# A recurrent layer with a gate: products of h added in PSUM onto x Wx and onto each other, a plain first step, and the gate's two layers moved

## The chip, the cores and the metric

The kernel runs on one core of a Trainium2 chip. The metric is the device time of one execution in microseconds (us). Before the change it is 3159.95 us, the median of three runs (3158.42 to 3160.47). The engines are named as in the profile: PE (TensorE), DVE (VectorE), ACT (ScalarE), POOL (GpSimd) and SP (SyncE, which here only issues DMAs).

## The reference

Layer 0 is a recurrence over 256 steps for 64 rows of width 1024, layer 1 a gate computed from the condition vector alone. All of it is float32.

```python
xW = jnp.einsum('ntd,dh->nth', x, Wx) + b          # x: (64, 256, 1024)
next_h = jnp.tanh(prev_h @ Wh + xw)                # 256 steps, h0 = cond
x = x + h_t
h = jax.nn.silu(cond @ W1.T + b1)
gate = jax.nn.sigmoid(h @ W2.T + b2)[:, None, :]
# v: a Haar transform over time, all coefficients times the gate, and its inverse
x = x + (v + a)
```

The transform is linear and its coefficients are all scaled by the same gate, so layer 1 is x times (2 + gate). The kernel calls that `factor`.

## The kernel before

Constants: S = 2 steps make a pair, NP = 128 pairs, T = 256 steps; P = 128, R = 32, Q = 4, B = 8, KB = 4, G = 2, W = 512, E = 128, D = 1024.

**x Wx.** For each pair of steps, `XWork` splits x into a high part x0, a rest x1 and a mixed part x2 (DVE lines 112, 244 and 246, ACT cast at line 252). PE multiplies them with three parts of Wx, 48 matmuls of 128 x 512 per pair (line 228). `first()` does the 16 "mixed" ones and 8 of "main", `second()` the other 24. ACT and POOL then take the mixed sums (lines 260 and 261, `+ b_row`), DVE adds the main sums (line 295), the pair goes to DRAM (`sum_d`, line 299) and comes back rearranged as xW of two steps (line 305, eight DMAs, four for each step), all issued by SP.

**h Wh.** Each step is a Strassen product in blocks of halves: seven products of 16 matmuls each (`strassen_product`, line 172; each float32 matmul stands as two records in the profile). The four column groups of the array work side by side on 32 columns of weights each. The weight sides are made once by `strassen_weight` (lines 159 to 162), the sides of h in every step by `strassen_sides` (lines 185 to 188). `h_product` runs products 1, 7, 5, 6, then 4, 3, 2. In PSUM, parts 7, 5, 4, 3 and 2 share the bank `three`, while m1 and m6 have their own. ACT copies m1 and the parts 5 and 7 out (lines 202 and 204), POOL makes four additions with xW (lines 208, 209, 210 and 213), DVE two more (lines 212 and 214), and line 218 adds `three` to y. Tanh is on ACT (line 392), the transposition of h on DVE (line 394).

**The loop.** For even steps PE gets, after the step's products, `second()` of the next pair; for odd steps `first()` of the pair after that. So between the last product of a step and the first of the next, PE has 24 matmuls of x Wx. Then POOL adds h to x (line 409).

**The gate.** In steps 0 to 7, `gate_product` adds one of eight blocks of the first layer (a load of a W1 slab and 8 matmuls of 256 columns, 16 records in the profile), in steps 8 to 15 the second layer. `gate_hidden` follows step 7 and `gate_factor` step 15. The biases b1 and b2 are loaded by ACT into the buffer of h0 (tag h0T), which has one copy.

**The output.** Until `factor` exists the first eight pairs are stored in DRAM (`kept`). Later pairs are scaled by POOL (line 379) and stored to yT. In pairs 9 to 16 the kept slabs are loaded, scaled on POOL and stored, one per pair.

**Preparation.** Ahead of the loop, x0 to x2 and the slabs of Wx and Wh are loaded by SP. Each Wx slab is split by DVE, ACT and, for odd k, POOL (`split_weight`, lines 112 and 123 to 126). Six buffers of 512 KB (tag slab) hold x, raw Wx and the gate's weights in turn.

The program names engines and data; a planner of the framework puts the instructions of each engine in order by its own costs, starting from the written order, and adds all waits. In the quiet pairs PE keeps the written order. In the preparation it doesn't: products of step 0 stand between blocks of x Wx. Several DVE instructions of `XWork` stand among the sides of h.

## Time and profile before

| quantity | value |
|---|---|
| median of 3 runs | 3159.95 us |
| profiled execution, in all | 3156.64 us |
| its span | 3154.8 us |
| mean granted PE clock | 0.995 |
| busy PE / DVE / ACT / POOL | 3098.7 / 2070.4 / 632.5 / 1703.2 us |
| moved by DMA | 303.85 MB, mean 96 GB/s |

The profile is of one execution. A row of a timeline has the start in us, the length in us, engine, line, operation, output and inputs, shapes and count, and in brackets the engine's idle time before it with what ended it. The chain of waits goes back from the last instruction to what released each one, and lists the pieces in order of time. A window row gives the stretch, its length, then the busy us (and instructions) of PE, PEld, DVE, ACT and POOL, the granted clock, the DMA share and GB/s.

### The profile page before, as it was taken

The page shows a single profiled execution, that of the slowest core. Times are in us where ns is not written, and L with a number is a line of the kernel's source. Part 1 is how long each engine was busy: PE and PEld are TensorE (multiplying, and loading weights), DVE is VectorE, ACT ScalarE, POOL GpSimd, SP SyncE. Part 2 cuts the span into 40 slices and gives each one's busy share as a digit, 9 for nine tenths or more (in the row PEclk, how much of TensorE's full clock was granted, in tenths as well). Part 3 has the DMA queues.
Part 4 walks back from the last instruction along what each step waited for, and adds up shares of the span by engine and source line. Part 5 has one row for each costly group of instructions (what it writes and reads, how often), then busy time and mean ns, then how long its engine had stood idle before and what let it go on. Part 6 is the DMA issues. An engine that isn't in the chain of part 4 may idle for free.

```text
span 3154.8 us, 138243 instructions
## 1 busy us (share of the span) xinstructions
PE 3098.7 (98%) x63744; PEld 2699.4 (86%) x63744; DVE 2070.4 (66%) x2722; ACT 632.5 (20%) x1172; POOL 1703.2 (54%) x1808
## 2 busy tenths in 40 slices
PE   6999999999999999999999999999999999999998
PEld 4878788888888888888888888888888888888887
DVE  7556566666676666666666666666666766666665
ACT  3111112122122122112211211221221211212121
POOL 4335655555555555555555555555555555555554
PEclk8999999999999999999999999999999999999999
DMA  5334332222222222222222222222222222222221
GB/s 185 128 118 143 120 116 95 90 89 90 96 82 95 95 84 93 93 89 89 89 96 83 93 93 89 90 95 90 89 89 96 83 94 96 85 90 95 90 74 65
DMA packets 145763, 303.85 MB, mean 96 GB/s; under 512 B 23584, under 2 KB 89632, under 8 KB 145184
## 3 DMA queue, kind: packets, MB, share of 16 engines
q1 hardware_dynamic: 144128, 293.69, 27.6%
q8 instruction: 500, 8.19, 1.1%
q10 hardware_dynamic: 1056, 1.31, 0.1%
q14 instruction: 79, 0.65, 0.1%
HBM read 156.50 MB, written 138.41 MB: 93 GB/s over the span
## 4 chain that ended last, share of the span: by engine, by line
PE 91%; DMA 2%; DVE 2%; issue 1%; POOL 1%; ACT 0%; SPq 0%; POOLq 0%; DVEq 0%; ACTq 0%
PE three L172 34%; PE main L228 28%; PE mixed L228 15%; PE m L172 14%; DMA kept_x<-kept 1%; DMA yT<-x 1%; PE ps_g L340 0%; DVE s L185 0%; POOL kept_x L379 0%; DVE x L244 0%; POOL x L409 0%; POOL y L213 0%; DVE hT L394 0%; DMA b_n<-b 0%; DMA sum_d<-sum 0%
## 5 line engine op out<-in xcount | busy, mean ns | idle before, releaser
L228 PE MATMUL main<-wx,x 128*128 128x512 f32 x4096 | 996.7, 395 | 19.0 <-ACT wx L123 14.6
L228 PEld LDWEIGHTS main<-wx,x 128*128 128x128 f32 x4096 | 759.9, 188 | 204.2 <-issue 26.8
L409 POOL TENSOR_TENSOR x<-x,hT 128x512 f32<-128x512 f32 x256 | 462.3, 1806 | 864.8 <-DVE hT L394 853.6
L172 PE MATMUL three<-wh,s 128*32 128x128 f32 x16320 | 544.6, 273 | 8.1 <-DVE s L185 5.7
L228 PE MATMUL mixed<-wx,x 128*128 128x512 f32 x2048 | 506.4, 399 | 1.3 <-DVE wx L126 0.9
L172 PEld LDWEIGHTS three<-wh,s 128*32 128x32 f32 x16320 | 459.0, 110 | 11.9 <-issue 10.6
L228 PEld LDWEIGHTS mixed<-wx,x 128*128 128x128 f32 x2048 | 375.7, 188 | 102.2 <-issue 25.8
L212 DVE TENSOR_TENSOR u<-m,c 128x128 f32<-128x128 f32 x256 | 74.5, 291 | 439.1 <-PE m L172 433.5
L392 ACT ACTIVATE h<-h 128x512 f32<-128x512 f32 x256 | 161.9, 633 | 1000.0 <-DVE h L218 1000.0
L218 DVE TENSOR_TENSOR h<-three,y 128x384 f32<-128x384 f32 x256 | 142.7, 558 | 334.5 <-PE three L172 304.0
L261 POOL TENSOR_TENSOR sum<-sum,b_row 128x512 f32<-128x512 f32 x256 | 341.7, 1336 | 6.2 <-ACT sum L260 6.2
L379 POOL TENSOR_TENSOR x<-x,factor 128x512 f32<-128x512 f32 x240 | 329.8, 1374 | 9.5
L394 DVE STREAM_TRANSPOSE hT<-h 128x512 f32<-128x512 f32 x256 | 182.0, 711 | 177.5 <-ACT h L392 177.5
L209 POOL TENSOR_TENSOR y<-c 128x128 f32<-128x128 f32 x256 | 127.3, 497 | 310.2 <-ACT c L204 310.2
L172 PEld LDWEIGHTS m<-wh,hT 128*32 128x32 f32 x8160 | 210.2, 110 | 94.0 <-issue 87.5
L172 PE MATMUL m<-wh,hT 128*32 128x128 f32 x8160 | 276.9, 277 | 6.9 <-DVE hT L394 6.8
L246 DVE SCALAR_TENSOR_TENSOR x<-x,x_high 128x1024 fp32r<-128x1024 f32 x128 | 282.6, 2208 | 0.0
L172 PE MATMUL three<-wh,hT 128*32 128x128 f32 x8160 | 274.8, 273 | 1.0 <-issue 0.4
L172 PE MATMUL m<-t,s 128*32 128x128 f32 x8160 | 269.8, 273 | 5.2 <-DVE s L187 5.2
L172 PE MATMUL three<-t,hT 128*32 128x128 f32 x8160 | 270.9, 273 | 2.0 <-ACT c L204 1.6
L172 PE MATMUL three<-t,s 128*32 128x128 f32 x8160 | 269.9, 273 | 0.0
L214 DVE TENSOR_TENSOR h<-y,u 128x128 f32<-128x128 f32 x256 | 202.0, 789 | 88.5 <-POOL y L210 87.5
(63 smaller groups left out, 3190.3 us busy)
## 6 DMA issues: line engine op xcount, KB each, us to landing
x<-xT SPq DMA_DIRECT2D x128, 512.0 KB, 3.8
sum_d<-sum SPq DMA_DIRECT2D x128, 512.0 KB, 3.0
xw<-sum_d SPq DMA_DIRECT2D x1024, 64.0 KB, 2.0
yT<-x SPq DMA_DIRECT2D x120, 512.0 KB, 2.8
wx<-wx SPq DMA_DIRECT2D x8, 512.0 KB, 7.0
wh<-wh SPq DMA_DIRECT2D x8, 512.0 KB, 5.8
w<-w1T SPq DMA_DIRECT2D x8, 512.0 KB, 3.9
kept<-x SPq DMA_DIRECT2D x8, 512.0 KB, 2.6
```

Source lines behind the costliest of these rows:

```text
L172: nc.tensor.matmul(out=out[q * R : (q + 1) * R], lhsT=a[:, k * R : (k + 1) * R], rhs=wh_s[i][k][:, q], start=first and k == 0, stop=k == K ...
L209: nc.gpsimd.tensor_add(y22, c57[:, 0], c57[:, 1])
L212: nc.vector.tensor_add(u, m6, c1)
L214: nc.vector.tensor_add(pre[:, 3], y22, u)
L218: nc.vector.tensor_add(pre[:, :3].rearrange("p i e -> p (i e)"), three[:, : 3 * E], y[:].rearrange("p i e -> p (i e)"))
L228: nc.tensor.matmul(out=acc[h], lhsT=v[:, k * P : (k + 1) * P], rhs=wx_s[k][which][:, h * HALF : (h + 1) * HALF], start=start and k == 0, s ...
L246: nc.vector.scalar_tensor_tensor(out=self.x2, in0=self.x1[:].bitcast(F32), scalar=-UP, in1=self.high, op0=ALU.mult, op1=ALU.add)
L261: nc.gpsimd.tensor_add(s, s, b_row[:, h * HALF : (h + 1) * HALF])
L379: nc.gpsimd.tensor_mul(v, v, blocks(factor))
L392: nc.scalar.activation(h, h, AF.Tanh)
L394: nc.vector.transpose(hT, h)
L409: nc.gpsimd.tensor_add(x_step(t), x_step(t), blocks(hT))
```

## The change

- `h_product` gets a PSUM bank `acc` into which ACT has copied xW of the step (`put`). Products 2, 4 and 3 are added onto it. Product 6 is added onto product 1 in the bank `m16`, after ACT has copied product 1 out to y0; ACT then copies the sum to u. Products 5 and 7 stand side by side in the bank `m57`. DVE makes y1, y2 and y3 from them and u, and one addition over 512 columns makes h. The four POOL additions, the copies c1 and c57 and the DVE sum of 128 columns are gone. The order of products is 1, 2, 5, 6, 7, 4, 3.
- Step 0 has a plain product of h0 with the raw Wh (64 matmuls of 256 columns) instead of a Strassen one; the Strassen sides of Wh are made afterwards, all on DVE.
- In the preparation, each of eight rounds loads a slab of Wx and one of W1 (SP) and one of Wh (ACT), splits Wx (the subtraction always on DVE), and gives PE a block of x Wx and a block of the gate's first layer.
- The gate's second layer is in steps 0 to 7; b1 has its own buffer, b2 that of h0. Three pairs are kept instead of eight; each is loaded in a pair with i % 4 = 0 and scaled in the next.
- Pairs are scaled by step. The last two steps are added and scaled by DVE in halves, with two stores on two queues.

```diff
-    def split_weight(w: bass.AP) -> list:
-        out = []
-        for k in range(B):
...
-            three = [wpool.tile([P, D], F32R, tag=f"wx{i}", name=f"wx{i}_{k}") for i in range(3)]
-            nc.scalar.copy(three[0], w0)
-            (nc.gpsimd if k % 2 else nc.vector).tensor_sub(raw, raw, w0)
...
-            out.append(three)
-        return out
-    def load_bias(v: bass.AP, name: str):
-        t = const.tile([P, G, F], F32, tag="h0T", name=name)
+    def split_weight(raw, k: int) -> list:
...
+        nc.scalar.copy(three[0], w0)
+        nc.vector.tensor_sub(raw, raw, w0)
...
+        return three
+    def load_bias(v: bass.AP, pool, tag: str, name: str):
+        t = pool.tile([P, G, F], F32, tag=tag, bufs=1, name=name)
...
-    def strassen_weight(raw: dict) -> dict:
+    def strassen_weight(raw: list) -> dict:
...
-            nc.gpsimd.tensor_sub(t1, b12, b11)
-            nc.gpsimd.tensor_sub(b12, b22, b12)
+            nc.vector.tensor_sub(t1, b12, b11)
+            nc.vector.tensor_sub(b12, b22, b12)
             nc.vector.tensor_sub(t2, b22, t1)
             nc.vector.tensor_sub(t4, b21, t2)
...
-    def strassen_product(out, a, i: int, first: bool) -> None:
+    def strassen_product(out, a, i: int, first: bool = False) -> None:
...
+    def plain_product(ps, vT, w, k: int) -> None:
+        for g in range(G):
+            col = (g * B + k) * R
+            for q in range(Q):
+                nc.tensor.matmul(
+                    out=ps[q * R : (q + 1) * R, g * F : (g + 1) * F],
+                    lhsT=vT[:, col : col + R],
+                    rhs=w[:, q * F : (q + 1) * F],
+                    start=k == 0 and g == 0,
+                    stop=k == B - 1,
+                    skip_group_check=True,
+                    tile_position=(0, q * R),
+                )
...
-    def h_product(a: dict, xw, t: int):
-        three = bank("three", f"three{t}")
-        m1, m6 = (bank(f"m{i}", f"m{i}_{t}")[:, :E] for i in (1, 6))
-        part = [three[:, i * E : (i + 1) * E] for i in range(3)]
-        pre = work.tile([P, 4, E], F32, tag="h", bufs=1, name=f"h{t}")
-        strassen_product(m1, a[1], 1, True)
-        strassen_product(part[2], a[7], 7, True)
-        strassen_product(part[1], a[5], 5, False)
-        strassen_product(m6, a[6], 6, True)
-        c1 = sums.tile([P, E], F32, tag="c1", name=f"c1_{t}")
-        nc.scalar.copy(c1, m1)
-        c57 = sums.tile([P, 2, E], F32, tag="c57", name=f"c57_{t}")
-        nc.scalar.copy(c57[:].rearrange("p i e -> p (i e)"), three[:, E : 3 * E])
-        y = sums.tile([P, 3, E], F32, tag="y", name=f"y{t}")
-        y22 = sums.tile([P, E], F32, tag="y22", name=f"y22_{t}")
-        nc.gpsimd.tensor_add(y[:, 0], c1, xw[:, 0])
-        nc.gpsimd.tensor_add(y22, c57[:, 0], c57[:, 1])
-        nc.gpsimd.tensor_add(y22, y22, xw[:, 3])
+    def flat(v):
+        return v[:].rearrange("p i e -> p (i e)")
+    def put(xw, t: int):
+        acc = bank("acc", f"acc{t}")
+        nc.scalar.copy(acc, flat(xw))
+        return acc
+    def h_product(acc, a: dict, t: int):
+        m16, m57 = (bank(f"m{i}", f"m{i}_{t}") for i in (16, 57))
+        m16, m5, m7 = m16[:, :E], m57[:, :E], m57[:, E : 2 * E]
+        part = [acc[:, i * E : (i + 1) * E] for i in range(3)]
+        y = sums.tile([P, 4, E], F32, tag="y", bufs=1, name=f"y{t}")
         u = sums.tile([P, E], F32, tag="u", name=f"u{t}")
-        nc.vector.tensor_add(u, m6, c1)
-        nc.gpsimd.tensor_add(y[:, 1:3], xw[:, 1:3], u[:].unsqueeze(1).broadcast_to((P, 2, E)))
-        nc.vector.tensor_add(pre[:, 3], y22, u)
-        strassen_product(part[2], a[4], 4, False)
-        strassen_product(part[1], a[3], 3, False)
-        strassen_product(part[0], a[2], 2, False)
+        strassen_product(m16, a[1], 1, True)
+        nc.scalar.copy(y[:, 0], m16)
+        strassen_product(part[0], a[2], 2)
+        strassen_product(m5, a[5], 5, True)
+        strassen_product(m16, a[6], 6)
+        nc.scalar.copy(u, m16)
+        strassen_product(m7, a[7], 7)
         nc.vector.tensor_add(
-            pre[:, :3].rearrange("p i e -> p (i e)"), three[:, : 3 * E], y[:].rearrange("p i e -> p (i e)")
+            y[:, 1:3], m57[:, : 2 * E].rearrange("p (i e) -> p i e", i=2), u[:].unsqueeze(1).broadcast_to((P, 2, E))
         )
-        return pre[:].rearrange("p i e -> p (i e)")
+        nc.vector.tensor_add(y[:, 3], m7, y[:, 1])
+        strassen_product(part[2], a[4], 4)
+        strassen_product(part[1], a[3], 3)
+        h = work.tile([P, W], F32, tag="h", bufs=1, name=f"h{t}")
+        nc.vector.tensor_add(h, acc, flat(y))
+        return h
     def bank(tag: str, name: str):
         return one_pool.tile([P, HALF], F32, tag=tag, name=name)
...
+        def block(self, k: int) -> None:
+            for h in range(2):
+                x_matmul(self.main, self.x0, 0, h, k, start=True)
+            for h in range(2):
+                x_matmul(self.main, self.x1, 1, h, k, stop=True)
+            for h in range(2):
+                x_matmul(self.mixed, self.x2, 2, h, k, True, True)
         def first(self) -> None:
             self.begin()
...
     nc.scalar.dma_start(out=h0T, in_=condT)
     b_row = const.tile([P, D], F32, tag="b_row", name="b_row")
-    nc.scalar.dma_start(out=b_row, in_=b.broadcast_to((P, D)))
     load_x(0)
     now = XWork(0)
-    wx_s = split_weight(wx)
+    now.begin()
+    gate_ps = bank("gate", "gate_ps1")
+    wx_s, wh_raw = [], []
+    for k in range(B):
+        raw = slab(f"wx{k}")
+        nc.sync.dma_start(out=raw, in_=wx[k])
+        w1 = slab(f"w1_{k}")
+        nc.sync.dma_start(out=w1, in_=w1T[k])
+        wx_s.append(split_weight(raw, k))
+        now.block(k)
+        plain_product(gate_ps, h0T, w1, k)
+        wh_raw.append(wpool.tile([P, D], F32, tag="wh", name=f"wh_{k}"))
+        nc.scalar.dma_start(out=wh_raw[k], in_=wh[k])
+        if k == 0:
+            nc.scalar.dma_start(out=b_row, in_=b.broadcast_to((P, D)))
+    b1_n = load_bias(b1, sums, "y", "b1_n")
     load_x(1)
-    wh_raw = load_by_halves(wh)
     load_x(2)
-    now.by_blocks()
+    now.take_mixed()
     xw_next = now.finish()
-    now = XWork(1)
-    now.first()
-    wh_s = strassen_weight(wh_raw)
-    gate_ps = {}
...
+    def gate_hidden(z):
+        nc.vector.tensor_add(z, gate_ps, z)
...
-    early = 2 * B // S
-    kept = [dram.tile([P, D], F32, tag="kept", bufs=early, name=f"kept{i}") for i in range(early)]
-    hT = h0T
-    sides = strassen_sides(hT, -1)
-    factor = None
+    def of_step(x, s: int):
+        return x[:].rearrange("p (b s g m) -> p s g b m", b=B, s=S, g=G)[:, s]
+    def scale(x, s: int) -> None:
+        nc.gpsimd.tensor_mul(of_step(x, s), of_step(x, s), blocks(factor))
+    acc = bank("acc", "acc0")
+    for k in range(B):
+        plain_product(acc, h0T, wh_raw[k], k)
+    h = work.tile([P, W], F32, tag="h", bufs=1, name="h0")
+    nc.vector.tensor_add(h, acc, flat(xw_next[0]))
+    now = XWork(1)
+    now.first()
+    g1T = gate_hidden(b1_n)
+    wh_s = strassen_weight(wh_raw)
+    kept, again, factor = [], [], None
     for t in range(T):
         i, s = divmod(t, S)
...
-        h = h_product(sides, xw[s], t)
+        if t:
+            h = h_product(acc, sides, t)
         nc.scalar.activation(h, h, AF.Tanh)
         hT = work.tile([P, W], F32, tag="hT", name=f"hT{t}")
         nc.vector.transpose(hT, h)
         if t + 1 < T:
             sides = strassen_sides(hT, t)
+        if s == 0:
+            acc = put(xw[1], t + 1)
...
             now = later
             now.first()
-        nc.gpsimd.tensor_add(x_step(t), x_step(t), blocks(hT))
+        if s == 1 and i + 1 < NP:
+            acc = put(xw_next[0], t + 1)
+        x = pairs[i]
+        if t + S < T:
+            nc.gpsimd.tensor_add(of_step(x, s), of_step(x, s), blocks(hT))
         if t < B:
-            gate_product(h0T, 0, t)
+            if t == 0:
+                gate_ps = bank("gate", "gate_ps2")
+            w2 = slab(f"w2_{t}")
+            nc.sync.dma_start(out=w2, in_=w2T[t])
+            plain_product(gate_ps, g1T, w2, t)
             if t == B - 1:
-                g1T = gate_hidden(load_bias(b1, "b1_n"))
-        elif t < 2 * B:
-            gate_product(g1T, 1, t - B)
-            if t == 2 * B - 1:
-                factor = gate_factor(load_bias(b2, "b2_n"))
+                factor = gate_factor(load_bias(b2, const, "h0T", "b2_n"))
+        if t + S >= T:
+            for half in range(2):
+                part = slice(half * KB, (half + 1) * KB)
+                v = of_step(x, s)[:, :, part]
+                nc.vector.tensor_add(v, v, blocks(hT)[:, :, part])
+                nc.vector.tensor_mul(v, v, blocks(factor)[:, :, part])
+                to = yT[i].rearrange("p (b s n) -> p s b n", b=B, s=S)[:, s, part]
+                (nc.sync, nc.scalar)[half].dma_start(
+                    out=to, in_=x[:].rearrange("p (b s n) -> p s b n", b=B, s=S)[:, s, part]
+                )
+        elif factor is not None:
+            scale(x, s)
+            if s == S - 1:
+                if t == B - 1:
+                    scale(x, 0)
+                nc.sync.dma_start(out=yT[i], in_=x)
+        elif s == S - 1:
+            kept.append(dram.tile([P, D], F32, tag="kept", bufs=B // S, name=f"kept{i}"))
+            nc.sync.dma_start(out=kept[i], in_=x)
         if s == S - 1:
-            if i < early:
-                nc.sync.dma_start(out=kept[i], in_=pairs.pop(i))
-            else:
-                scale(pairs[i])
-                nc.sync.dma_start(out=yT[i], in_=pairs.pop(i))
+            del pairs[i]
             if i + 3 < NP:
                 load_x(i + 3)
-        elif early < i <= 2 * early:
-            j = i - early - 1
-            x = slab(f"kept_x{j}")
-            nc.sync.dma_start(out=x, in_=kept[j])
-            scale(x)
-            nc.sync.dma_start(out=yT[j], in_=x)
+        if factor is not None and kept and i >= B and i % 4 < 2:
+            if i % 4 == 0 and s == 0:
+                again = slab(f"again{i}")
+                nc.sync.dma_start(out=again, in_=kept[0])
+            elif i % 4 == 1:
+                scale(again, s)
+                if s == 1:
+                    nc.sync.dma_start(out=yT[i // 4 - B // 4], in_=again)
+                    kept.pop(0)
 
```

## The prediction

> **What bounds the kernel now.** I read the page's busy times first. The first line is each engine's busy time, the second TensorE's share in 40 slices.
>
> ```profile
> PE 3098.7 (98%) x63744; PEld 2699.4 (86%) x63744; DVE 2070.4 (66%) x2722; ACT 632.5 (20%) x1172; POOL 1703.2 (54%) x1808
> PE   6999999999999999999999999999999999999998
> ```
>
> TensorE has no room except at the two ends. The change keeps its matmuls (seven products of 112 matmuls per step, 48 of x Wx per pair), so a gain must come from time in which TensorE is not at its pace. The chain of waits finds it: the start of `second()`, "main x24", comes once per pair of steps (start us, length us, what).
>
> ```profile
> 65.54 5.65 PE main L228 x24
> ...
> 91.24 5.71 PE main L228 x24
> ...
> 116.88 5.71 PE main L228 x24
> 122.58 1.00 PE ps_g L340 x16
> ...
> 142.70 5.71 PE main L228 x24
> ...
> 162.54 4.44 DMA b_n<-b
> 167.00 3.23 DMA b_n<-b
> ...
> 198.90 5.67 PE main L228 x24
> ...
> 251.54 5.71 PE main L228 x24
> ...
> 270.63 3.74 DMA kept_x<-kept
> 274.53 2.52 POOL kept_x L379 x2
> ```
>
> ```profile
> 460.07 5.66 PE main L228 x24
> ...
> 1511.24 5.66 PE main L228 x24
> 1535.06 5.66 PE main L228 x24
> ...
> 3089.40 5.66 PE main L228 x24
> ```
>
> A quiet pair takes 1535.06 - 1511.24 = 23.83 us with rounding. From 65.54 to 3089.40 there are 125 pairs: 3023.9 us, 45.1 more than 125 x 23.83 = 2978.8. It divides so: a gate block adds (116.88 - 91.24 - 23.83)/2 = 0.9 us, 16 of them 14.4; the two pairs from 142.70 to 198.90 take 56.2 against 51.3 with their gate blocks, 4.9 for the late bias; 251.54 to 460.07 is 208.5 for 8 pairs, less 190.6 and two gate blocks: 16.1 for slabs that were put aside; the 110.3 quiet pairs lose 8.0 in scattered small gaps; about 1.5 elsewhere. In front lie 65.5 us of preparation, behind 65.4 us of end.
>
> The windows by stage show that the 16.1 is a stall and not work: here TensorE is busy 196.2 of 208.5 us, afterwards 2627.5 of 2629.3 (columns: us, then busy us of PE, PEld, DVE, ACT, POOL, then clock, DMA share, GB/s).
>
> ```profile
> 251.54:460.07 208.53, 196.20 (x4002) 168.61 (x4001) 127.91 (x171) 38.79 (x73) 128.08 (x126) 1.00 0.38 128
> 460.07:3089.40 2629.33, 2627.49 (x54561) 2307.06 (x54561) 1754.56 (x2310) 526.39 (x990) 1442.61 (x1540) 1.00 0.27 90
> ```
>
> **The change, part by part.**
>
> *Preparation, -10.4 us.* The new order of TensorE is: eight blocks of x Wx, each with a gate block; the plain first step; `first()`; then `second()`. VectorE sets the pace of the blocks: one slab's three operations took 9.73 to 13.03, 3.30 us, when GpSimd was silent (1.23 for the subtraction), but 2.27 to 2.75 for single ones beside GpSimd. With all on VectorE and GpSimd idle, 8 x 3.30 from 9.73 ends at 36.1. Loads: x, h0, the bias row, 8 Wx, 8 W1 and 8 Wh are 13.9 MB; at the 345 to 420 GB/s of the busy stretches 33 to 40 us, the last Wx a little before the end. Slabs are scarce: W1 takes buffers that Wx had, and a Wx load waits for an earlier gate block. I take 40 for the last split. TensorE: last block 1.5 and its gate block 0.9 (42.4), plain first step 64 matmuls = 8 gate blocks x 0.87 = 7.0 (49.4), `first()` 5.7: `second()` starts at 55.1, not 65.54. Bounds: last split at 36 gives -14.4; at 50, nothing (before, the last Wx split ended at 52.6). I take the value nearer to the first, as the rows of 3.30 and of the loads agree there. Below nothing is possible (second rival).
>
> VectorE could be late instead: after 40 it has the split of x1 (3.2), two sums (1.4), h (0.7), the hidden gate layer (2.1), a transposition (0.7), sides (1.0), and 16 Strassen subtractions at 0.68 (10.9) that were half GpSimd's: 20.0, to 60.0. The first Strassen step starts on TensorE at 55.1 + 5.7 + 0.9 = 61.7 (72.19 before). So 1.7 us of cover; beyond it each late us costs one. The eight Wh loads and the bias row now go out from ScalarE, 9 issues at about 0.45 among work of 2.1 us per block (1.04 + 1.06): within the 3.3. Sigmoid's table load (1.28) moves here too, beside `first()`.
> xW of step 0: from the last mixed matmul to its use took 54.4 to 66.3; from 41.5 this is 53.4, before `first()` ends.
>
> *Gate, -7.2 us and -4.9 us.* Eight of 16 gate blocks leave the loop: 8 x 0.9. The 4.9 goes because b1 no longer waits for the buffer of h0, which the gate itself was reading (DMA b_n at 162.54). b2 takes that buffer at step 7; it has been free since step 0. If its eight issues stand in a row on ScalarE (4.78 us before), the copies behind them are late: y0, and so product 6; `put`, and so product 2. Bounds 0 and 4.9. ScalarE idles 2.3 us before the copy c1 and y0 has 1.2 us to spare: 4.8 - 3.5 = 1.3, so I take +1.5. The w2 loads stay on SP's queue, where a gate load stood between `sum_d` and xW before (99.25 between 98.83 and 101.77) without holding TensorE up.
>
> *Slabs put aside, -16.1 us.* Three slabs instead of eight; `again` is loaded one pair ahead and scaled in the next. What made the stall was GpSimd's order: the scaling of `kept_x` waited 22.0 us for its load with the additions for y queued behind it, and h waited for y. The change takes all four additions of `h_product` off GpSimd, so h no longer hangs there. Next late would be the second `sum + b_row`, in the quiet pair done at 1530.7, 10 us ahead of its use. Bounds: all 16.1, or none if the scaling holds up that sum.
>
> *The step itself, 0.* New on ScalarE: `put` (512 columns: 0.60 to 0.63 by the rows of mixed and tanh), y0 and u (0.27 each); c1 and c57 (0.27, 0.37) go. VectorE: h grows from 384 to 512 columns, 0.56 to 0.69 (the gate's sum); u 0.29 and the 128-column h 0.79 go; y1,2 costs about 0.43 (between 0.29 and 0.56) and y3 0.29. The chain from the last product to hT, 0.2 + 0.69 + 0.63 + 0.71 = 2.4 us with handoffs, stands under 24 matmuls of 5.66. New waits on TensorE, with its order 1, 2, 5, 6, 7, 4, 3: product 6 waits for y0's copy, covered by products 2 and 5 (1.75 us against about 0.5; without cover each 0.1 us would cost 25); product 2 waits for `put`; behind them in TensorE's queue is the whole step. The close one is `put` for even steps, which needs xW of the new pair. The timeline of before:
>
> ```profile
> 1522.63 4.64 SPq L305 DMA_DIRECT2D xw<-sum_d  x8
> 1527.04 0.60 ACT L260 ACTIVATE sum<-mixed 128x512 f32<-128x512 f32 x1 [1.22 <-PE mixed L228]
> 1529.64 1.06 PE L172 MATMUL three<-wh,s 128*32 128x128 f32 x32
> 1529.95 0.27 ACT L202 COPY c<-m 128x128 f32<-128x128 f32 x1 [2.31 <-PE m L172]
> ```
>
> Half of the eight issues end at 1524.95, landing takes 2.0: 1526.95. ScalarE is free at 1527.64, `put` ends at 1528.3; the second product starts at 1529.64. Margin 1.3 us, so 0. The DMAs of the step keep their places on SP's queue; the added load of `again` and its store come once in four pairs, while SP's queue is free from 1532.4 to the next `sum_d` at 1543.7.
> If ACT's write into PSUM cost twice the row, 0.6 more, it would still fit.
>
> The Trainium skill's page "PSUM — Partial Sum Buffer" (Summary: rules for kernel authors) speaks against this part: a ScalarE seed other than 0 is to go through TensorE or be added after evacuation. By that rule I would add one matmul of 512 columns per step, an estimate of 255 x 0.236 (5.66/24) = 60 us; the diff holds no such matmul, and no run here shows the bits, so the sum leaves it out.
>
> *End, -0.5 us.* The last two steps run exposed: h dearer by 0.13, three times, +0.4. After hT (3147.8), GpSimd's 1.25 and 1.26 give way to four half operations of about 0.42 on VectorE and two half stores: -0.9.
>
> Sum: -10.4 - 7.2 - 4.9 + 1.5 - 16.1 + 0 - 0.5 = -37.6. The profiled execution, 3154.8 of span and 3156.64 in all, becomes 3119.0. It lies 3.3 below the median of 3159.95; for the median I say 3122.
>
> **Rivals.**
> *Preparation gains nothing.* For: W1 and Wh add loads while only six slabs exist, and TensorE ran single blocks at half clock there (1.22 us for a pair of matmuls against 0.73). Against: the stretches of 0.12 to 0.49 DMA share between 15 and 30 us show room. Then 3122 + 10 = 3132; with 12 us lost, 3144.
> *The slabs still stall* or b2 costs fully: + 16.1 or + 3.4: 3138.
> *`put` is late (slower).* The planner that orders each engine's queue could place `put` behind y0's copy (1529.95 to 1530.22), or on odd steps behind the cast of x0 (1516.94 to 1517.99). Product 2 then starts near 1530.9, 1.2 late: 127 x 1.2 = 152, 3274. It decides from (37.6 + 6.3)/127 = 0.35 us per pair beyond the margin of 1.3. Against: `put` is written ahead of y0's copy, and TensorE followed the written order in the quiet pairs.
> *The page's rule above is right for the time*: not counted, since it would be other code.
>
> **How the numbers follow.** Forecast 0.64, preparation without gain 0.17, slabs or bias still stalling 0.06, `put` late 0.13. No change is about 0.2%, 6.3 us. The first three are faster, except some 0.03 of the second near no change: faster 0.84, same 0.03, slower 0.13. The forecast's own range is 3108 (preparation -14.4, b2 free, scattered gaps smaller by 8) to 3131; for 8 in 10 I go to 3144, the preparation's loss, leaving out `put` and tails: 3106 to 3144.
>
> **What would show it.** Right: `second()` of the first pair near 55, pairs of 23.83 from the loop's ninth step on, no wait of TensorE for ACT's `put`, GpSimd under 1250 us busy (its four additions sum to 555). Wrong: TensorE idle at product 2 once per pair; the first `second()` after 65; pairs over 25 between steps 8 and 34.

## The result, and the profile after

The changed kernel takes 3130.91 us (median, 3130.0 to 3132.18), the kernel before in four runs 3159.18 (3156.17 to 3160.47): a ratio of 0.9912, with a 95% interval from 0.9895 to 0.9929. It is faster, by 28 us or 0.9%. The forecast was 3122, the range 3106 to 3144. The time lies next to the rival "preparation gains nothing", 3132. The profiled execution took 3132.18 us with a span of 3130.4, against 3156.64 and 3154.8 before: 24.4 us less.

The page of the changed kernel, busy times:

```profile
PE 3090.0 (99%) x63648; PEld 2696.5 (86%) x63648; DVE 1762.4 (56%) x2736; ACT 717.9 (23%) x1425; POOL 1112.9 (36%) x768
```

TensorE has as much to do as before. GpSimd lost 590 us of work and VectorE 308, ScalarE got 85 more; none of that is time by itself. The time is in the distances of `second()`, "main x24" or x26 in the chain of waits of the changed kernel (start us, length us, what):

```profile
66.43 5.90 PE main L237 x26
...
76.98 1.51 issue
94.21 5.71 PE main L237 x24
107.01 0.81 issue
...
122.46 5.67 PE main L237 x24
...
149.87 5.68 PE main L237 x24
...
178.09 5.66 PE main L237 x24
...
444.94 5.66 PE main L237 x24
...
3090.43 5.66 PE main L237 x24
```

Three readings. The first `second()` starts at 66.43 and not near 55: the preparation gave nothing. The four pairs up to 178.09 take 27.4 to 28.3 us where a pair with two gate blocks should take 25.6; a new stall stands in them, pieces of "issue" of 0.3 to 1.5 us. From 444.94 to 3090.43 there are 111 pairs of 23.83: here nothing is lost any more, while before 8.0 us were lost in small gaps. The windows row of that stretch (length, then busy us of PE, PEld, DVE, ACT, POOL, clock, DMA share, GB/s) shows the same, TensorE busy for all but 0.06 us:

```profile
460.00:3080.00 2620.00, 2619.94 (x54555) 2304.29 (x54554) 1477.34 (x2307) 600.31 (x1210) 961.88 (x660) 1.00 0.27 90
```

Against the terms of the forecast, by the two profiled executions (after minus before, us):

| term | forecast | measured |
|---|---|---|
| preparation (start of the first `second()`) | -10.4 | +0.9 |
| eight gate blocks fewer in the loop | -7.2 | -7.2 |
| biases b1 and b2 | -3.4 | -2.8 |
| slabs put aside (pairs of the loop up to 445) | -16.1 | -11.4 |
| scattered gaps and odds in other pairs | 0 | -9.1 |
| new "issue" pieces in the pairs with gate blocks | 0 | +7.0 |
| end | -0.5 | -1.6 |
| sum | -37.6 | -24.2 |

The spans differ by 24.4; 0.2 is rounding. The second row is by the same price of 0.9 per block; the third counts what the pair from 66.43 loses beyond its two blocks (27.78 - 23.83 - 1.8 = 2.1) against the 4.9 before; the fourth is what three pairs with a slab lose now (1.86, 1.36 and 1.47, together 4.7) against 16.1. All this is one execution. In a second profile of the changed kernel, taken with the last runs, the first `second()` starts at 63.30, and the three pairs with a slab lose 4.75, 0.74 and 3.80, together 9.3 instead of 4.7. Three runs below with the same preparation (one slab of W2, the copy twice and four times) start the loop at 63.35, 63.96 and 67.68. So that start is known to about 4 us only; the missing gain in the preparation is 8 to 13, and the gain on the slabs is 7 to 11.

Why the preparation gained nothing is read from its chain:

```profile
30.26 6.69 DMA w<-w1T
...
48.62 0.35 ACTq L133
...
49.48 1.05 ACT wx L123
...
54.76 0.61 ACT sum L269
...
55.44 2.14 POOL sum L270
...
57.60 0.70 DVE sum L301
...
58.35 2.93 PE main L237 x6
```

and from the waits of the same kernel between 40 and 66 us (who waited for whom: us in total, times, longest):

```profile
DVE b_n L345 <- PE gate_ps L180: 4.9, 1, 4.9
ACT wx L123 <- DVE b_n L345: 4.7, 1, 4.7
```

The loads of W1 stand in the chain. Then the gate's own sum (`z`, line 345) sits in VectorE's queue ahead of the last splits of Wx and waits 4.9 us for the gate's last product; on ScalarE the issues of b2's load (line 133) wait for the buffer of h0 and stand ahead of the last copies of Wx (line 123). The last split ended at 54.2, the forecast had 40. At the end, `first()` waits for the main banks (58.35): sums on ScalarE, GpSimd and VectorE, 3.6 us without cover. The forecast had put the plain first step there, but TensorE had done it in the waits for loads.

A third thing is in VectorE's busy time. The windows row of the stretch of the splits (the fifth column is VectorE), first of the changed kernel, then of the run with one slab of W1 below:

```profile
14.00:54.20 40.20, 34.39 (x268) 15.76 (x265) 33.44 (x40) 16.71 (x16) 0.00 (x0) 0.96 0.83 293
```

```profile
13.50:47.30 33.80, 28.56 (x237) 13.32 (x229) 33.41 (x40) 16.84 (x16) 0.00 (x0) 0.92 0.76 252
```

The work is the same 33.4 us, and 15 of the 40 instructions are Strassen subtractions for Wh (0.68 each): the planner put them between the splits, and the forecast had them all behind. So even with hardly an idle moment the splits end at 47.4.

### The profile page after: what moved, and what is told of

The parts are those of the page before. It is cut to its first block, busy times and chain, and to the rows that moved or that the text cites. A ratio compares the mean times of both kernels' runs of the same rounds, so it can differ in the third digit from the quotient of the medians.

```text
span 3130.4 us, 137359 instructions
## 1 busy us (share of the span) xinstructions
PE 3090.0 (99%) x63648; PEld 2696.5 (86%) x63648; DVE 1762.4 (56%) x2736; ACT 717.9 (23%) x1425; POOL 1112.9 (36%) x768
## 4 chain that ended last, share of the span: by engine, by line
PE 97%; DMA 1%; DVE 1%; issue 0%; ACT 0%; SPq 0%; POOL 0%; ACTq 0%; DVEq 0%
PE main L237 30%; PE m L163 29%; PE acc L163 21%; PE mixed L237 16%; DMA w<-w1T 1%; PE gate_ps L180 1%; DMA xw<-sum_d 0%; DVE h L229 0%; DMA h0T<-condT 0%; ACT h L393 0%; DVE hT L395 0%; DVE s L195 0%; DVE s L193 0%; DVE s L194 0%; PE acc L180 0%
## 5 line engine op out<-in xcount | busy, mean ns | idle before, releaser
L222 DVE TENSOR_TENSOR y<-m,u 128x256 f32<-128x256 f32 x255 | 108.2, 424 | 865.6 <-PE m L163 865.6
L163 PE MATMUL m<-t,s 128*32 128x128 f32 x16320 | 494.2, 273 | 2.4 <-DVE s L195 2.4
L163 PEld LDWEIGHTS m<-t,s 128*32 128x32 f32 x16320 | 452.4, 110 | 3.0 <-issue 2.9
L229 DVE TENSOR_TENSOR h<-acc,y 128x512 f32<-128x512 f32 x255 | 176.4, 692 | 243.5 <-PE acc L163 243.5
L163 PE MATMUL acc<-wh,s 128*32 128x128 f32 x8160 | 272.6, 273 | 2.9 <-issue 2.9
L163 PE MATMUL acc<-t,hT 128*32 128x128 f32 x8160 | 270.5, 273 | 2.1 <-issue 2.1
L163 PE MATMUL acc<-wh,hT 128*32 128x128 f32 x8160 | 271.4, 274 | 1.0 <-ACT acc L205 0.9
L163 PE MATMUL m<-wh,s 128*32 128x128 f32 x8160 | 269.9, 273 | 0.0
L261 ACT CAST x<-x_high 128x1024 fp32r<-128x1024 f32 x128 | 134.0, 1047 | 472.6 <-PE main L237 471.0
L163 PEld LDWEIGHTS acc<-wh,s 128*32 128x32 f32 x8160 | 229.6, 110 | 4.4 <-issue 4.4
```

Of the source, the lines that this page charges most:

```text
L163: nc.tensor.matmul(out=out[q * R : (q + 1) * R], lhsT=a[:, k * R : (k + 1) * R], rhs=wh_s[i][k][:, q], start=first and k == 0, stop=k == K ...
L222: nc.vector.tensor_add(y[:, 1:3], m57[:, : 2 * E].rearrange("p (i e) -> p i e", i=2), u[:].unsqueeze(1).broadcast_to((P, 2, E)))
L229: nc.vector.tensor_add(h, acc, flat(y))
L261: nc.scalar.copy(self.x0, self.high)
```

## Experiments

**The preparation: loads or queues.** Three theories: the bytes (L), two waits that stand in the queues ahead of the splits (W), or the work on VectorE (V). The first run takes 3.5 MB away: one slab of W1 is loaded and used for all eight blocks, so the gate's first layer is computed with wrong weights.

```diff
-        w1 = slab(f"w1_{k}")
-        nc.sync.dma_start(out=w1, in_=w1T[k])
+        if k == 0:
+            w1 = slab("w1_0")
+            nc.sync.dma_start(out=w1, in_=w1T[0])
```

> The changed kernel with one W1 slab loaded and used for all eight gate blocks of the preparation, so its gate is computed from the wrong weights; seven loads of 0.52 MB less. Theory L (the preparation is held up by its loads): 3.7 MB at about 400 GB/s are 9 us, the first second() starts near 58 instead of 66.4, and the time falls by 7 to 9 us, to about 3123. Theory W (it is held up by two waits in the order of the queues, both for the last gate block): the last gate block comes a little earlier, 1 to 4 us, and the start stays above 62. Theory V (VectorE's own work sets the pace): no change.

Measured: 3123.93 us (3122.45 to 3125.11), ratio 0.9894 (0.9880 to 0.9909), span 3122.3. The second run keeps every byte and takes the two waits away: b2 gets its own buffer, and the gate's sum stands behind the first step's sum on VectorE.

```diff
-                factor = gate_factor(load_bias(b2, const, "h0T", "b2_n"))
+                factor = gate_factor(load_bias(b2, sums, "b2", "b2_n"))
...
-    g1T = gate_hidden(b1_n)
+    with tc.issue_after(h_add.ins):
+        g1T = gate_hidden(b1_n)
```

> The changed kernel with b2 in a buffer of its own, and with the three VectorE operations of the hidden gate layer queued behind the sum that makes h of step 0. Theory W: ScalarE no longer stands from 43.7 to 49.4 at the issue of b2, nor VectorE from 43.7 to 48.6 at the gate's sum; the last Wx split ends near 48.5 instead of 54.2, the first second() starts near 61, and the time falls by 5 to 6 us, to about 3125. Theory L: the last Wx slab lands when it did, and the time falls by at most 2 us. Theory V: no change.

Measured: 3126.13 us (3124.74 to 3130.97), ratio 0.9906 (0.9889 to 0.9922), span 3123.6; the last split ended at 50.6. The `second()` of pair 1 came at 94.21 in the changed kernel (91.08 in its second profile); in these two runs, chain of waits:

```profile
86.09 5.71 PE main L237 x24
```

```profile
61.06 5.89 PE main L237 x26
88.41 5.85 PE main L237 x24
```

The first is the run with one slab of W1, the second the one without the two waits. The loop starts 5 to 8 us earlier with fewer bytes and 3 to 6 earlier without the waits. The time of the second overlaps with that of the changed kernel, so its gain rests on the traces: five profiles with the two waits start the loop at 63.30 to 67.68, three without them (61.06 here, 59.07 and 61.02 in two kernels below) at 59.07 to 61.06. Both count, and neither is the whole; the two can't be added either, since with fewer bytes the gate's sum doesn't wait any more (41.83 us, without idle time). What is left then is VectorE's own work. Whether the place of W1 matters rather than its bytes was the question of a later run. It starts from the kernel "W2 apart" below and loads W1 behind Wx and Wh, its products behind `first()` of pair 1:

```diff
-        w1 = slab(f"w1_{k}")
-        nc.sync.dma_start(out=w1, in_=w1T[k])
...
-        plain_product(gate_ps, h0T, w1, k)
...
     now.first()
+    for k in range(B):
+        w1 = slab(f"w1_{k}")
+        nc.sync.dma_start(out=w1, in_=w1T[k])
+        plain_product(gate_ps, h0T, w1, k)
```

> As the run before it, and the slabs of W1 are loaded behind Wx and Wh, their products behind the first half of pair 1. Theory L (the 4 MB of W1 between the slabs of Wx hold the split back): the split ends some 4 to 8 us earlier, but the 128 products of 7.2 us and the gate's sum then stand near the end of the preparation: 0 to 6 us less than the run before, 3113 to 3120. Rival (all of x, Wx, Wh and W1 must be there before the loop, so their order buys nothing): within 1 us of the run before, or some us more, as the products no longer lie in the waits for loads.

Measured: 3127.22 us (3120.45 to 3129.55), ratio 0.9895 (0.9879 to 0.9912), against 3122.89 (3120.49 to 3127.58) of the kernel it starts from. The times overlap; the chain tells more:

```profile
58.69 2.72 PE gate_ps L180 x46
61.41 5.64 PE main L239 x24
...
71.06 1.28 ACT L346
```

Without the 2.7 us of gate products `second()` would start at 58.7; it starts at 59.07 in the kernel with W1 between the slabs. So the place of W1 bought nothing, and the gate's products, its sum and the 1.28 of ScalarE ahead of the sigmoid now stand in the first step: pair 0 takes 92.84 - 61.41 = 31.4 us instead of 27.5. The rival held.

**The new "issue" pieces.** In steps 0 to 7 a slab of W2 is loaded right ahead of the store of the sum (even steps) or the load of x (odd steps): two transfers of 512 KB at one time, and a few us later TensorE has a gap for which the profile names no releaser. Here one slab of W2 is loaded and used eight times, so the gate's second layer is computed with wrong weights.

```diff
-            w2 = slab(f"w2_{t}")
-            nc.sync.dma_start(out=w2, in_=w2T[t])
+            if t == 0:
+                w2 = slab("w2_0")
+                nc.sync.dma_start(out=w2, in_=w2T[0])
```

> The changed kernel with one W2 slab loaded and used for all eight gate blocks of steps 0 to 7, so its gate is computed from the wrong weights. Theory B (TensorE's gaps of 0.6 to 1.4 us that the chain calls issue, in steps 2 to 7, come from its instructions being fetched while a W2 load and the store of sum are in the DMA engines together): the three pairs from 94 to 178 us fall from 28.0 to 25.6 us each, the time by about 7 us, to 3124. Rival (the gaps belong to the instruction stream with the gate blocks, whatever is moved): nothing changes, 3131 within 2.

Measured: 3123.05 us (3121.17 to 3124.84), ratio 0.9892 (0.9877 to 0.9906), span 3119.3. Its chain:

```profile
73.89 1.52 issue
91.14 5.71 PE main L237 x24
...
167.18 0.43 issue
169.12 5.69 PE main L237 x24
```

The three pairs from 91.14 to 169.12 take 78.0 us, in the changed kernel 83.9 (94.21 to 178.09): 5.9 less, where three quiet pairs and six gate blocks make 76.9. Of six gaps one of 0.43 is left. Another 3.1 us of the difference in span lie ahead of the first `second()` (63.35), in a part that this edit doesn't touch: the second profile of the changed kernel has 63.30 there. The 1.5 at 73.89 stays, so it isn't from these loads.

Is it the number of bytes or their coming together? In the next run all eight slabs are loaded again, but by ScalarE, two for the next pair in each odd step: one behind the copy of u, one behind tanh. It has the edits of the run without the two waits, too.

```diff
-        nc.scalar.copy(u, m16)
+        u_copy = nc.scalar.copy(u, m16)
+        if t % S and t + 1 < B:
+            load_w2(t + 1, u_copy)
...
-        nc.scalar.activation(h, h, AF.Tanh)
+        tanh = nc.scalar.activation(h, h, AF.Tanh)
+        if t == 0:
+            load_w2(0, tanh)
+            load_w2(1, tanh)
+        elif s == 1 and t + 2 < B:
+            load_w2(t + 2, tanh)
```

> The changed kernel, whole, with b2 in a buffer of its own and the gate's sum behind the first step's sum on VectorE (as in the run without the two waits, 3126), and the slabs of W2 loaded by ScalarE's queue in the odd steps of the pair before, one behind its copy of u and one behind its tanh, no longer next to the store of the sum and the load of x. Theory B (TensorE's issue gaps come from loads that follow each other closely): four pairs take 26 us each instead of some 27.5, 6 to 8 us less than 3126: 3118 to 3121. Rival (the gaps come from the mere number of bytes): 3125 to 3128.

Measured: 3122.89 us (3120.49 to 3127.58), ratio 0.9890 (0.9876 to 0.9905), span 3118.6. The same three pairs:

```profile
86.54 5.71 PE main L239 x24
...
165.37 5.68 PE main L239 x24
```

That is 78.8 us with every byte loaded, 5.1 less than the changed kernel and 4.1 less than the run without the two waits (83.0, from 88.41 to 171.38), against 5.9 when seven slabs are left out. So the number of bytes isn't the cause. The edit changes the place of the loads and their queue together; which of the two does it isn't told apart. That the gaps are late instructions of TensorE, as the theory had it, no run shows; shown is that most of them are gone when the loads no longer stand next to other transfers on SyncE's queue.

**The slabs put aside: the step or the scaling.** The forecast said that h hung on GpSimd's additions for y, and that taking these off GpSimd would end the stall. The chain of waits of the kernel before bears out the first half. One of the eight pairs:

```profile
300.18 3.14 DMA kept_x<-kept
...
303.46 1.28 POOL kept_x L379
304.74 0.71 POOL y L213
...
305.47 0.57 DVE h L218
...
306.73 0.71 DVE hT L394
...
308.54 1.27 DVE s L185
```

The load of the slab, its scaling, y, h, its transposition and a side s follow one another. The waits of that stretch, VectorE's for y and TensorE's:

```profile
DVE h L218 <- POOL y L213: 30.5, 6, 6.2
PE m L172 <- DVE s L187: 5.2, 7, 0.8
PE three L172 <- DVE s L185: 4.4, 5, 1.3
PE m L172 <- DVE hT L394: 2.2, 3, 0.9
```

The next kernel is the one before with the changed step (`put` and the new `h_product` from step 1) and nothing else; eight slabs are still put aside.

> The kernel before with the new step only: put, the new h_product and its order from step 1 on; preparation, gate, kept slabs and end are those of before. Forecast's theory: the stall of pairs 7 to 14 goes, because h no longer hangs on GpSimd, 16 us, and with the 8 us of scattered gaps that were no part of the forecast up to 24: 3135 to 3143. Rival (what was left of the stall in the changed kernel, 1.5 us for each kept slab, comes from VectorE's sides beside GpSimd's scaling): eight slabs still cost 12, so 4 of the 16 are gained, with the scattered gaps 12: about 3147. If the stall is the queue of SP and not GpSimd: 3151 or more.

Measured: 3151.15 us (3144.31 to 3156.38), ratio 0.9975 (0.9965 to 0.9985). The stall is still there, with no addition for y left on GpSimd: the eight pairs from 250.93 to 459.25 take 208.3 us, as before (208.5). What the step alone did end is the small gaps: its 111 pairs from 459.25 to 3105.25 take 23.84 each. TensorE's waits in the eight pairs name the copy of x Wx into the bank (and through it the load of x Wx), and a difference of s:

```profile
PE acc L172 <- ACT acc L229: 9.7, 6, 2.9
PE m L172 <- DVE s L187: 1.2, 1, 1.2
```

So x Wx came late. Why? GpSimd may slow VectorE's sides and sums (D), or the slab's transfers may hold SyncE's queue (Q). Two runs from the kernel with the step alone were to tell them apart. One loads and stores each slab but doesn't multiply it by the factor, so that these outputs lack it:

```diff
             x = slab(f"kept_x{j}")
             nc.sync.dma_start(out=x, in_=kept[j])
-            scale(x)
             nc.sync.dma_start(out=yT[j], in_=x)
```

> The kernel before with the changed step, and the eight slabs put aside are loaded again and stored again but not multiplied by the factor (those outputs lack it). The step alone left their stall: its pairs from 250.93 to 459.25 took 208.3 us, where eight quiet pairs of 23.84 make 190.7, 17.6 more. Theory D (GpSimd's scaling slows VectorE beside it: a difference of s 1.38 instead of 0.28, x2 2.31 instead of 1.22; so the sum is stored late, Wx x comes late and the copy into the bank is late): the stall goes, the eight pairs take 191 to 194, and the time falls from 3151 by 14 to 18 to 3133 to 3138. Theory Q (the slab's load and store stand ahead of the loads of x Wx on SyncE's queue): the stall stays, 3149 to 3153.

The other scales each slab as before, but loads it one pair ahead:

```diff
-        elif early < i <= 2 * early:
...
+        if early <= i <= 2 * early:
+            if s == S - 1 and i < 2 * early:
+                again = slab(f"kept_x{i - early}")
+                nc.sync.dma_start(out=again, in_=kept[i - early])
+            if s == 0 and i > early:
+                scale(again)
+                nc.sync.dma_start(out=yT[i - early - 1], in_=again)
```

> The kernel before with the changed step, and each slab put aside is loaded one pair ahead, so that its scaling can start at once in its pair. Theory D: GpSimd scales as much beside VectorE as before, the stall stays in size, if not in place: 3147 to 3154. Theory Q: the load no longer holds the queue or GpSimd, the stall goes at least by half, 3133 to 3143.

Measured: without the scaling 3135.09 us (3133.51 to 3135.53), ratio 0.9932 (0.9916 to 0.9949); with the early load 3145.85 (3139.11 to 3150.58), ratio 0.9969 (0.9958 to 0.9980). The windows rows of the stretch with slabs, first of the step alone, then without the scaling, then with the early load:

```profile
250.93:459.25 208.32, 196.95 (x4002) 170.73 (x4001) 114.76 (x171) 43.47 (x89) 88.65 (x62) 0.98 0.37 126
```

```profile
255.00:455.00 200.00, 199.15 (x4143) 174.32 (x4145) 117.20 (x180) 45.55 (x91) 70.01 (x48) 1.00 0.38 134
```

```profile
252.15:455.49 203.34, 194.16 (x4002) 168.34 (x4001) 112.19 (x171) 43.59 (x89) 89.72 (x62) 1.00 0.37 129
```

The second column is the length, the third TensorE's busy time. Without the scaling TensorE idles 0.85 of 200 us at the same DMA share; with the early load still 9.2 of 203.3, against 11.4 of 208.3. So the stall hangs on the scaling. The early load gained nothing clear: its times overlap with those of the step alone. But the runs don't tell D from Q. On SyncE's queue the slab's store waits for the scaling, in the run with the early load too, and without the scaling both ways are gone. So the pairs have to be looked at one by one. In the timeline of the step alone, one pair:

```profile
283.14 3.01 POOL L412 TENSOR_TENSOR kept_x<-kept_x,factor 128x512 f32<-128x512 f32 x2 [0.51 <-DMA kept_x<-kept]
283.64 1.37 DVE L187 TENSOR_TENSOR s<-s,hT 128x128 f32<-128x128 f32 x1
...
286.93 0.32 SPq L332 DMA_DIRECT2D sum_d<-sum  x1
...
296.00 0.59 ACT L229 COPY acc<-xw 128x512 f32<-128x512 f32 x1 [5.67 <-DMA xw<-sum_d]
```

Beside the scaling of the slab a difference of s takes 1.37 instead of 0.28. (The 2.31 for x2, which the expectation of the run without the scaling names, is no mark of the slab: in a quiet pair of the changed kernel x2 takes 2.30, beside the scaling of x.) A sum of main, which reads PSUM and one SBUF operand, keeps its 0.68 while GpSimd scales (284.93). This agrees with the Trainium skill, page "SBUF — State Buffer" (Who interferes with whom): a VectorE instruction with two SBUF inputs contends with a GpSimd instruction that reads SBUF, one with at most one such input, outside the two-port modes, doesn't. The lengthening of 1.09 is about one GpSimd multiplication (1.3 to 1.5 each here). `second()` began at 276.50 here, so the sum's store goes out 10.4 us after it; in a quiet pair of the changed kernel it is 8.8 (1493.61 to 1502.39). The copy starts 19.5 after `second()` instead of 16.9 (1.6 by the late store, the rest in the transfers), and product 2, due at 18.4, waits for it. That is theory D. Of the eight pairs it is so in two, from 276.50 and 329.78; the first has no loss. In the other five it is the queue. The pair from 380.50:

```profile
387.77 0.34 SPq L468 DMA_DIRECT2D yT<-kept_x  x1
...
389.11 0.68 DVE L328 SCALAR_TENSOR_TENSOR sum<-main,sum 128x512 f32<-128x512 f32 x1
...
392.45 0.33 SPq L108 DMA_DIRECT2D x<-xT  x1
392.88 0.38 SPq L332 DMA_DIRECT2D sum_d<-sum  x1
```

VectorE's last sum ends at 389.8, 9.3 us after `second()` (8.8 in a quiet pair), but its store goes out at 392.88. Ahead of it on the queue stands a load of x, and the profile has that load wait for the slab's store to land (seven such waits in the eight pairs, 20.8 us). In these five pairs the sum is ready 1.2 to 3.7 us before its store. So the scaling delays the store of the sum in two ways: by VectorE in two pairs, and through the slab's store, a load of x behind it and the order of SyncE's queue in five.

**The margin of `put`.** The copy is made twice, then four times, at each step.

```diff
-        nc.scalar.copy(acc, flat(xw))
+        for _ in range(4):
+            nc.scalar.copy(acc, flat(xw))
```

> The changed kernel with the copy of x Wx into the bank made twice (0.59 us each), at both steps of a pair. In a quiet pair of the changed kernel the copy of the odd side starts at 1510.51 and takes 0.59, and product 2 starts at 1512.02: 0.9 us are free. Theory M (margin of 0.9 us): nothing, 3131 (3129 to 3134), quiet pairs 23.83. Rival (the copy already sets the pace, or the bank comes free too late): 0.4 to 0.6 us for each of 120 pairs, 3180 to 3200.

> The changed kernel with the copy of x Wx into the bank made four times. Theory M: 1.77 us more ScalarE time less the 0.9 that are free is 0.9 us for each of some 120 pairs: 105 us more, 3215 to 3260, and TensorE waits for the copy of the odd side in the quiet pairs. Rival (more is free than that, since product 2 can be put behind others): under 3180.

Measured: 3137.26 us (3135.75 to 3138.77), ratio 0.9941 (0.9921 to 0.9961), for two, and 3203.03 (3201.58 to 3204.49), ratio 1.0149 (1.0129 to 1.0169), for four. TensorE's waits for the copy were 0.9 us in the changed kernel; with two copies they are 8.8 us in 11 steps; with four:

```profile
PE acc L163 <- ACT acc L206: 50.9, 63, 2.6
```

Both expectations miss: two copies cost 6 to 9 us against the two sets of runs of the changed kernel (3.5 by the spans), not nothing, and four cost 72 to 75, not 105. The margin isn't one number. With four copies TensorE waits at only 63 of 255 steps, and other pairs still take 23.83. In the pair from 1493.6 of the changed kernel the copy could start 16.9 us after `second()`, in the pair from 1501.87 with four copies 15.0 after it: x Wx comes back sooner or later from pair to pair by 2 us. A margin read from one pair (0.9 or 1.3) is one sample of that.

**All of it together.** The last kernel joins the two edits of the preparation, W2 apart, and one against the rest of the slabs' stall: each of the three slabs is scaled by halves, behind GpSimd's addition in the odd steps of two pairs, where VectorE has least to do. The changed kernel ran once more beside it.

```diff
-            elif i % 4 == 1:
-                scale(again, s)
-                if s == 1:
+            elif i % 4 and s == 1:
+                with tc.issue_after(added.ins):
+                    scale(again, i % 4 - 1)
+                if i % 4 == 2:
                     nc.sync.dma_start(out=yT[i // 4 - B // 4], in_=again)
```

> The changed kernel as it is, on the same chip as the run after it, so that the two can be compared: 3131 (3129 to 3133).

> The changed kernel, whole, with b2 in its own buffer, the gate's sum behind the first step's sum, W2 loaded apart from the other transfers, and each slab put aside scaled by halves in the odd steps of two pairs instead of at one go. Theory D (GpSimd beside VectorE's even step is what the three pairs with a slab lose, 1.86, 1.36 and 1.47 in the changed kernel): these pairs take 23.9 to 24.2, 3 to 5 us less than the 3122.9 of W2 apart: 3118 to 3121, 10 to 13 below the changed kernel. Rival (the late x Wx there comes from the slab's load and store on SyncE's queue): 3122 to 3124.

Measured: 3117.50 us (3114.59 to 3119.51), ratio 0.9878 (0.9865 to 0.9892); the changed kernel beside it 3128.10 (3125.93 to 3132.95), ratio 0.9912 (0.9898 to 0.9925). The intervals lie apart: 10.6 us less than the changed kernel by the medians. Its chain has no pair with a loss after the gate:

```profile
191.83 5.66 PE main L239 x24
...
453.94 5.66 PE main L239 x24
```

Between these lie eleven pairs of 23.83, the slabs' pairs among them. In the kernel with W2 apart the same stretch still had three pairs with 1.4 to 1.6 too much, 4.5 us. So it matters where the scaling, and with it the slab's store, stands. Which of the two ways counts this run doesn't tell: in all these pairs VectorE's sums end in time, 8.8 us after `second()` or sooner, and their store follows at once. In the changed kernel both ways occur. In its first profile TensorE waits twice for a difference of s, 1.2 us each; in its second it waits three times for the copy, 5.3 us, and in the pair from 222.87 the sum is ready at 231.0 and its store goes out at 235.31, behind a load of x.

## Why the prediction was right, and where not

The sign, the range and most of the loop held; the forecast was 9 us too low. That it is no farther off is partly luck: by the table +11.3 in the preparation, +7.0 in new pieces, +4.7 on the slabs and +0.6 on the biases stand against -9.1 of small gaps and -1.1 at the end, which the sum did not have either. Two of its signs of being wrong showed, too: the first `second()` came after 65 (66.43), and two pairs after step 8 took over 25 (25.7 of the 49.5 from 201.92 to 251.44, and one of 25.3 before 444.94).

- **Preparation: failed.** "I take 40 for the last split" was the wrong step; it was 54.2. The sum gave VectorE 3.30 for each split and put the 16 Strassen subtractions behind the last one; 15 of them stand in the stretch of the splits, and with these VectorE needs until 47.4 even without waits. The other 7 us are idle time of VectorE, 4.9 of it for the gate's last product: the gate's sum on VectorE and b2's issues on ScalarE stood in the queues ahead of the last splits. The forecast had placed b2's load at step 7; it is written there, but the planner moved it forward to where its buffer comes free. The loads count through that product, which waits for W1. Their mean rate up to 40 us was 326 GB/s in the first profile and 347 in the second, which started the loop at 63.30 all the same. So the rival "preparation gains nothing" came true, and its reason (loads for which only six slabs exist) is a part of the cause. Its other reason, TensorE at half clock, isn't borne out: the windows row from 15 to 20 us of the kernel before, with a 1.22 at 17.32, grants a clock of 1.00.
- **Gate, -7.2: right.** The blocks are gone from the loop, and pairs of 23.83 begin after the slabs. The price of 0.9 is the forecast's own; no run takes the blocks out alone. b1's stall of 4.9 is gone. b2 did not cost its 1.5 at step 7, but stood in the preparation. In its place the first pair loses 2.1 (1.51 of it in one "issue" piece); what causes that stays open.
- **W2's loads: missed.** "Without holding TensorE up" was read from one pair of before (99.25 between 98.83 and 101.77). After the change the three pairs with these loads take 4 to 6 us more than with the loads set apart or left out; they come together with another 512 KB in each of the eight steps.
- **Slabs put aside: right in sign, -11.4 (-6.8 by the second profile) instead of -16.1.** The reading of the kernel before was right: the wait for the load, the scaling, y and h are on its chain in six of the eight pairs. The wrong step was from there to "so h no longer hangs there", and thus to no stall. With no addition for y on GpSimd the stall stayed as long as it was, 208.3 us, since the store of the sum came late in its place, by VectorE or by SyncE's queue. That the two lengths agree is chance. The bound "none if the scaling holds up that sum" named the place, though not the queue. The gain goes with three slabs in place of eight; no run shows that alone.
- **The step, 0: its terms right, its gain missed.** y1,2 took 0.424 (0.43 forecast), h 0.692 (0.69), `put` 0.58 to 0.59. Product 6 never waits. The step alone took 7 of the 8 us of small gaps away (0.9 are left in 111 pairs), which the forecast had left standing and only used for the lower end of its own range (its "110.3 quiet pairs" are 110; only with 110 do 8.0 come out); why these gaps were there in the kernel before isn't settled. GpSimd is at 1112.9, below the 1250 asked for.
- **`put` late: did not happen**, 0.9 us of waiting in all. The rival's price was real, though: with more ScalarE work ahead of product 2 the kernel becomes slower than before.
- **The page's rule on the seed.** The Trainium skill, page "PSUM — Partial Sum Buffer" (The four PSUM rules; the summary has it shorter, as a seed that must be 0), would send a ScalarE seed other than 0 through TensorE or add it after evacuation. Here the seeding is a ScalarE copy of 0.59, TensorE has 96 records fewer than before and no matmul for it, and the estimated 60 us are not there.
- **End, -0.5:** it measured -1.6.

## What to carry to other kernels

For a stall that you mean to remove, follow its chain, and then ask what else in that stretch hangs on the same transfer or operation: with one way closed, the next can be as long, here through a store and the order of a DMA queue. When work moves into a phase that was waiting for loads, look for every instruction that can stand in a queue ahead of the last useful one, also those written later, and count it in. Spread transfers and a helper engine's work over the steps in which the suppliers of the bounding engine are idle: here that gave 4 to 5 us and 4.5 us in the traces, beside the 24 that the change itself gave there.

## What the runs showed of the hardware that was not expected

- TensorE lost 0.3 to 1.4 us at a time, with no releaser in the profile, in steps where a 512 KB load was issued next to another transfer of that size; with the same loads set apart on another queue, three pairs took 78.8 us instead of 83.9.
- VectorE beside GpSimd: a subtraction of 128x128 took 1.37 instead of 0.28, and through the store and reload of x Wx this reached TensorE some 13 us later (283.64 to 296.64). A 128x1024 operation took 2.30 beside GpSimd, and one of the same shape 1.22 in the preparation, where GpSimd is idle.
- The preparation of one and the same kernel ended at 66.43 in one profile and at 63.30 in another, while the quiet pairs of both take 23.83.
